# A graph layer on one core: the first node tile made alone, its own small table, the bias product after that of h, and counts that get ahead over 20 steps

## The chip, the cores and the metric

The kernel runs on one core of one Trainium2 chip. A core has TensorE (PE, with weight loads as PEld), VectorE (DVE), ScalarE (ACT), GpSimd (POOL) and SyncE (SP, which here only issues DMAs). The metric is device microseconds of one execution. The median of three runs of the kernel before is 5252.87 us (5247.94 to 5257.49).

## The reference

Node features `x` (12500 x 128) go through a graph layer with a residual. There are 412500 edges, sorted by destination node `dst`:

```
h    = relu(layernorm(x)) @ W_in2f
Wij  = (ssp(f_ij @ W_f1 + b_f1) @ W_f2 + b_f2) * rcut_ij      # 20 -> 128 -> 128 per edge
agg  = segment_sum(h[dst] * Wij, src)                          # idx_j = dst, idx_i = src
out  = x + ssp(agg @ W_o1 + b_o1) @ W_o2 + b_o2                # ssp(z) = softplus(z) - log 2
```

Since `dst` is sorted, the rows of h that 512 edges in a row need lie close together: about 15.5 nodes per 512 edges. The sources are in no order, so the messages have to be spread over all nodes.

## The kernel before, in words

**Making h.** `make_h(q)` (L332) makes h for a quad of four tiles of 128 nodes, in steps parted by `yield`: load of x, statistics (DVE, and two activations on ACT); scaling (DVE); transposes (PE) and relu (ACT); product with `win` (PE) and first bfloat16 part (ACT); the rest after that part (`left`, DVE) and second part (ACT); third part (DVE) and stores. Three bfloat16 parts stand for one float32. The stores go to HBM tables (`tables`, L129): table 0 holds the first quad, the others overlapping stretches, and a chunk reads from the one that `table_of` names (0 for chunks 0 to 8), so that it can read before later quads are there.

**Edges in chunks.** A chunk is 512 edges, a group four chunks; there are 806 chunks. For chunk k the following is issued. `rows` (L614): SP reads a start row from `shifts` into a register and loads 32 rows of the h table (`near`). `window` (L757): DVE compares relative destinations (`rel`, loaded per group in twelve-step advance) with row numbers, giving 0/1 matrices `at`. `pick` (L775): PE multiplies `at` by `near`, giving h rows for the edges; ACT scales them by rcut (`picked`, L784, gives `hg`). `hidden`, `hidden_log`, `hidden_end` (L663 to L685): the first layer of the edge net, two chunks at a time, on PE, ACT (three activations) and DVE (`r`). `value` (L764): second layer on PE, with the bias product of `ones_b` and `bf12_p` last in the sum. `message` (L793): DVE multiplies `v` and `hg` into `o`, and POOL scatters it to HBM by four indirect DMAs, one per 128 edges. Slots of the scatter come from counts: `blocks` (L687, DVE, `inb`), `rank` (L695, PE, sum over the edges so far in `free`), `rank_end` (L712, DVE, `top` and, for the first three groups, three small operations per chunk). `free` is one PSUM tile that each count adds to, so a count waits for `rank_end` of the one before.

**Collecting.** Slots are zeroed ahead in segments (L1127). After each segment, `Collect` (L818) loads them, compares and adds them up on DVE and PE beside later chunks; the last segment and the output layer (`finish`) come after the last scatter.

**Order.** The whole program is written out in order by hand (`manual_schedule`, L1096): each engine and each DMA queue runs its instructions in program order. Before the loop come `constants` (L254), the first quad, and the pieces of chunk 0. Then `step(k)` (L954) from k = -1 issues what is due: `part(name, upto, make)` makes all chunks up to a limit. In step k the message is that of k, pick and value are those of k + 1, hidden that of k + 4. For k under 10 (`steady` false) the end of the counts (`slots`) comes ahead of the message, later after it; the count limit `upto` (L1001) grows by half a chunk more per step until it is 6 ahead. After each step both first `make_h` generators move on by one step; from k = 6 (`NEXT - 3` is 5) `side` makes the later quads, one per nine steps, and the starts and relative destinations of later chunks. `rows` are held back to chunk `NEXT` until the second quad is stored.

`biases` and `bias_parts` (L304, L311) form the fixed second-layer bias b_f1 W_f2 + b_f2 (the hidden layer is kept without b_f1, which `nbf1` and this product make up for) and cut it into three bfloat16 rows of `bf12_p`.

Of the kernel before, what the change touches and what calls it, by code (L numbers as in the profile page):

```python
# [41 lines left out]
def gnn_kernel(  # L42
# [84 lines left out]


    tables = [(0, QN)]  # L129
# [4 lines left out]
    for c in range(NC):  # L134
        n = c * CH * N // n_edges
        table_of.append(0 if n < QN - NEAR - P else min(n // QN, NQ - 1) + 1)
# [46 lines left out]
    def load_x(q):  # L183
        n = min(QT, NTILE - q * QT)
        full = min(n, N // P - q * QT)
        xb = ln.tile([P, QT, P], F32, name="xb")
        if full < n:
            nc.vector.memset(xb[:, full:n, :], 0.0)
            nc.sync.dma_start(xb[:N % P, full, :], x[q * QN + full * P:N, :])
        if full:  # L190
            nc.sync.dma_start(xb[:, :full, :], x[q * QN:q * QN + full * P, :]
# [62 lines left out]
    def constants():  # L254
# [3 lines left out]
        first_load(0)  # L258
        nc.sync.dma_start(win, w_in2f)

        for j in range(NCHUNK):
            nc.sync.dma_start(wf1[32 * j:32 * j + RBF, :], w_f1)

        nc.scalar.preload_act_table_set("natural_log_exp_and_others")
        nc.scalar.dma_start(bf1, b_f1[:, None])
        nc.scalar.dma_start(wf2, w_f2)
        nc.scalar.dma_start(bf2, b_f2[None, :].to_broadcast([P, P]))
# [4 lines left out]
        prow_i = early_room[:WP, rows_at + 5 * NC:rows_at + 5 * NC + 1].bitcast(I32)  # L272
# [7 lines left out]
        nc.gpsimd.memset(ones_b, 1.0)  # L280
        nc.gpsimd.memset(bf12_p, 0.0)
# [9 lines left out]
        nc.vector.memset(bad, 0.0)  # L291
        nc.vector.memset(rel[:, NPART - 1, :], 0.0)
        nc.vector.memset(ones, 1.0)
        nc.vector.memset(none, 0.0)

        for t in range(QT):
            nc.vector.memset(turn[:, :, t:t + 1], -1.0 if t % 2 else 1.0)
        nc.vector.tensor_scalar(prow_i, prow_i, 7, None, op0=ALU.logical_shift_right)
        nc.vector.tensor_copy(prow, prow_i)
# [3 lines left out]

    def biases(psum):  # L304

        nc.vector.tensor_scalar(nbf1, bf1, -1.0, None, op0=ALU.mult)
        b12 = psum.tile([P, QT, P], F32, name="b12", tag="acc")[:, 0, :]
        nc.tensor.matmul(b12, bf1.to_broadcast([P, P]), wf2, start=True, stop=True)
        nc.vector.tensor_add(bf12, b12, bf2)

    def bias_parts():  # L311

        left = bf12[:3, :]
        for k in range(3):
# [926 lines left out]
```

## Time and profile before

| what | value |
|---|---|
| median of three runs | 5252.87 us |
| the profiled execution's own time | 4236.61 us |
| its span, first to last instruction | 4234.9 us |
| mean granted TensorE clock | 0.882 |
| POOL busy | 3095.9 us (73%), 3246 instructions |
| PE, DVE, ACT busy | 3371.9 us (80%), 3352.9 us (79%), 2329.8 us (55%) |
| DMA moved | 820.92 MB, mean 194 GB/s |
| first and last scatter start | 26.1 and 4106.6 us |

The profile is one execution; its own time is 1016 us less than the median of the runs, so durations from it are set against its own time. A row of the table of groups gives line, engine, operation, output and inputs, then the busy total in us, the mean ns of one instruction, and the engine's idle time just before them with what ended most of it. A timeline row gives start and duration in us, then in brackets the idle time before it and its releaser; `SPq` are DMA issues on SP. "issue" is time in which the engine waited for nothing that the profile shows. DMA issue rows show issuing time only, landing comes later.

### The profile page before, as it was taken

The numbers are of one execution on the slowest core, as the hardware profiler recorded it, in microseconds if no ns is written. First come the engines' busy times: TensorE is split into PE (matmuls) and PEld (weight loads), VectorE is DVE, ScalarE is ACT, GpSimd is POOL, SyncE is SP. The second block draws the span as 40 slices with busy tenths as digits, with TensorE's granted clock in tenths as the row PEclk, the third lists the DMA queues.
The fourth block names the chain that finished last, engine by engine and source line by source line (L and its number), as shares of the span: only waits on it lengthen the run. The fifth ranks groups of instructions, "written<-read, shape, count | busy, mean of one in ns | idle before, by whom it ended". The sixth has DMA issues, their size and how long they took to land. (4 is left out here: it accounts for less than half of the span.)

```text
span 4234.9 us, 73728 instructions
## 1 busy us (share of the span) xinstructions
PE 3371.9 (80%) x22378; PEld 2543.6 (60%) x22378; DVE 3352.9 (79%) x6752; ACT 2329.8 (55%) x4686; POOL 3095.9 (73%) x3246
## 2 busy tenths in 40 slices
PE   6766666666666666689998899898898988888888
PEld 4444444444444444467777777777776777767777
DVE  8877766776666656678888888888888998999978
ACT  5665565655555555555555555555555555555535
POOL 5777777777777777777777777777777777777760
PEclk9877877877777777789999999999999999999999
DMA  5765555555444454366787777877787768767667
GB/s 171 213 192 180 176 175 177 157 159 159 126 118 132 121 164 125 107 193 210 229 269 213 216 212 211 267 229 218 214 243 234 229 203 270 234 203 204 184 183 232
DMA packets 515591, 820.92 MB, mean 194 GB/s; under 512 B 177075, under 2 KB 312871, under 8 KB 515187
## 3 DMA queue, kind: packets, MB, share of 16 engines
q1 hardware_dynamic: 411586, 602.85, 49.2%
q0 software_dynamic: 103168, 213.15, 15.3%
q8 instruction: 181, 2.97, 0.3%
q14 instruction: 224, 1.83, 0.1%
q10 hardware_dynamic: 432, 0.13, 0.0%
HBM read 419.09 MB, written 396.64 MB: 193 GB/s over the span
## 5 line engine op out<-in xcount | busy, mean ns | idle before, releaser
L804 POOL DMA_INDIRECT slots<-o,slot x3224 | 3092.5, 959 | 1010.8 <-issue 770.3
L769 PE MATMUL v<-wf,r 128*128 128x128 f32 x6448 | 1066.6, 317 | 540.7 <-DVE o L800 539.1
L769 PEld LDWEIGHTS v<-wf,r 128*128 128x128 f32 x6448 | 924.7, 221 | 590.3 <-DVE o L800 571.2
L789 ACT ACTIVATE hg<-picked,rcut 128x128 f32<-128x128 f32 x3224 | 907.7, 368 | 630.9 <-PE picked L780 292.5
L866 PEld LDWEIGHTS acc<-to,m 128*128 128x128 f32 x8132 | 1017.2, 201 | 235.9 <-issue 142.0
L866 PE MATMUL acc<-to,m 128*128 128x128 f32 x8132 | 1078.8, 289 | 32.5 <-DVE to L853 22.1
L675 ACT ACTIVATE a<-z,bf 128x1024 f32<-128x1024 f32 x403 | 450.4, 1118 | 853.5 <-PE z L668 853.0
L668 PE MATMUL z<-f,wf 20*128 20x512 f32 x1612 | 527.2, 734 | 224.8 <-DVE r L684 223.3
L853 DVE TENSOR_TENSOR to<-count_ps,m 128x512 f32<-128x512 f32 (+3 forms) x824 | 641.8, 804 | 65.6 <-DMA m<-slots 34.7
L800 DVE TENSOR_TENSOR o<-v,hg 128x512 f32<-128x512 f32 x806 | 550.5, 683 | 48.8 <-PE v L771 25.0
L798 DVE COPY o<-place 128x8 f32<-128x8 f32 x403 | 77.0, 191 | 610.6 <-DMA slots<-o,slot 609.9
L760 DVE TENSOR_TENSOR at<-count_ps,rel 96x512 bf16<-96x512 f32 x806 | 545.7, 677 | 0.0
L684 DVE SCALAR_TENSOR_TENSOR r<-z,nbf,a 128x1024 f32<-128x1024 f32 x403 | 513.9, 1275 | 21.1 <-ACT a L677 21.1
L677 ACT ACTIVATE a<-a,half 128x1024 f32<-128x1024 f32 x403 | 462.8, 1148 | 13.1
L713 DVE TENSOR_REDUCE top<-free 128x4 f32<-128x392 f32 x806 | 446.7, 554 | 8.1 <-PE free L708 8.1
L689 DVE TENSOR_TENSOR inb<-count_ps,blk 128x392 f16<-128x392 f32 x806 | 447.4, 556 | 0.0
L676 ACT ACTIVATE a<-a 128x1024 f32<-128x1024 f32 x403 | 426.0, 1057 | 12.8
L780 PEld LDWEIGHTS <-at 96*128 96x128 bf16 x3224 | 256.0, 105 | 251.1 <-DVE at L760 104.0
L668 PEld LDWEIGHTS z<-f,wf 20*128 20x128 f32 x1612 | 138.8, 210 | 409.6 <-DVE r L684 362.2
L780 PE MATMUL picked<-near,at 96*128 96x128 bf16 x3224 | 343.2, 234 | 32.1 <-DVE at L760 26.8
L771 PE MATMUL v<-bf_p,ones_b 128*128 128x512 bf16 x806 | 353.3, 438 | 0.0
L741 PE MATMUL free<-inb,rest_of 128*128 128x392 f16 x806 | 302.9, 376 | 12.6 <-DVE top L713 12.6
(112 smaller groups left out, 1428.2 us busy)
## 6 DMA issues: line engine op xcount, KB each, us to landing
m<-slots SPq DMA_DIRECT2D x311, 387.0 KB
m<-slots SPq DMA_DIRECT2D x317, 258.0 KB
rel<-rel_d SPq DMA_DIRECT2D x202, 384.0 KB
m<-slots SPq DMA_DIRECT2D x172, 322.5 KB
slots<-o,slot POOLq DMA_INDIRECT x3224
slots<-zero SPq DMA_DIRECT2D x96, 387.0 KB
slots<-zero SPq DMA_DIRECT2D x64, 516.0 KB
f<-in_f_t SPq DMA_DIRECT2D x404, 80.0 KB
```

The costliest lines, as they stand in the source:

```text
L668: nc.tensor.matmul(z[:, k, :], wf1[rows, :], self.f[rows, :], start=True, stop=True)
L675: nc.scalar.activation(a, z, AF.Abs, bias=bf1)
L677: nc.scalar.activation(a, a, AF.Ln, bias=half, scale=0.5)
L684: nc.vector.scalar_tensor_tensor(r, z, nbf1, a, op0=ALU.max, op1=ALU.add)
L760: nc.vector.tensor_tensor(at, prow_ps.to_broadcast([WP, CH]), self.rel[:, c, :], op=ALU.is_equal)
L769: nc.tensor.matmul(v[:, i, :], r[:, i * P:(i + 1) * P], wf2, start=i == 0, stop=False, skip_group_check=True)
L780: nc.tensor.matmul(ps[:, i, :], at[:, i * P:(i + 1) * P], near, start=True, stop=True)
L789: nc.scalar.activation(hg[:, i, :], ps[:, i, :], AF.Copy, scale=self.rcut[:, j:j + 1])
L800: nc.vector.tensor_mul(o[:, :, :P], v, hg)
L804: put = nc.gpsimd.indirect_dma_start(out=views[j % VIEWS], out_offset=bass.IndirectOffsetOnAxis(ap=self.slot[:, j:j + 1], axis=0), in_=o[: ...
L853: nc.vector.tensor_tensor(to[:, :n, :], count_ps[:, None, :].to_broadcast([P, n, P]), self.m[u][:, :n, P:].to_broadcast([P, n, P]), op=ALU ...
L866: nc.tensor.matmul(self.acc[b // QT][:, i, :], m[:, j, :P], to[:, j, :], start=t == 0, stop=t == self.seg.tiles(b) - 1)
```

## The change

The first `make_h` makes one tile, the second the other three of the first quad, the third and later ones a quad each (`made_h`). A new table 0 holds the first tile's 128 rows and serves chunks 0 to 4; the first quad's table serves chunks 5 to 22; later tables are as before, numbered one higher. `served()` gives the last chunk whose table has been stored in program order, in place of `NEXT`. Of the constants, `win` and two of the four copies of `w_f1` are loaded by ACT's queue; `wf2`, `bf2`, the first destinations, the next three tiles of x and the other two copies move to SP behind the first group's source indices, and the first `rel` store and load behind the statistics. DVE's constants move into `more_constants` and `window_rows`, and three memsets to the late loads. `bias_parts` is gone: the bias product comes after h's on PE, and its three parts are cut on all partitions, with `ones_b` now zero but for rows 0, 32 and 64. `shift` comes after h is stored. In the loop the non-steady form lasts 20 steps, the window and the counts get ahead over those 20 steps, the third `make_h` starts at step 4, and the side work at step 12. What is computed stays the same.

```diff
-    tables = [(0, QN)]
+    made_h = [(0, 1), (1, QT - 1)]
+    made_h += [(t, min(QT, NTILE - t)) for t in range(QT, NTILE, QT)]
+    tables = [(0, P), (0, QN)]
...
     table_of = []
     for c in range(NC):
         n = c * CH * N // n_edges
-        table_of.append(0 if n < QN - NEAR - P else min(n // QN, NQ - 1) + 1)
+        table_of.append(0 if n <= P - 2 * WR else 1 if n < QN - P - WR
+                        else min(n // QN, NQ - 1) + 2)
...
         early[0] = load_x(0)
         part_load(0)
-        first_load(0)
-        nc.sync.dma_start(win, w_in2f)
-        for j in range(NCHUNK):
-            nc.sync.dma_start(wf1[32 * j:32 * j + RBF, :], w_f1)
         nc.scalar.preload_act_table_set("natural_log_exp_and_others")
+        nc.scalar.dma_start(win, w_in2f)
+        for j in range(2):
+            nc.scalar.dma_start(wf1[32 * j:32 * j + RBF, :], w_f1)
         nc.scalar.dma_start(bf1, b_f1[:, None])
...
-        nc.gpsimd.memset(ones_b, 1.0)
-        nc.gpsimd.memset(bf12_p, 0.0)
+        nc.gpsimd.memset(ones_b, 0.0)
+        for k in range(3):
+            nc.gpsimd.memset(ones_b[32 * k:32 * k + 1, :], 1.0)
...
+    def more_constants():
+        nc.vector.scalar_tensor_tensor(after, ident, BIG, after, op0=ALU.mult, op1=ALU.add)
+        nc.vector.tensor_scalar(rest_of, after, -1.0, 1.0, op0=ALU.mult, op1=ALU.add)
+        for t in range(QT):
+            nc.vector.memset(turn[:, :, t:t + 1], -1.0 if t % 2 else 1.0)
         nc.vector.memset(bad, 0.0)
+    def window_rows():
+        nc.vector.tensor_scalar(prow_i, prow_i, 7, None, op0=ALU.logical_shift_right)
+        nc.vector.tensor_copy(prow, prow_i)
+    def biases(psum):
+        b12 = psum.tile([P, QT, P], F32, name="b12", tag="acc")[:, 0, :]
+        nc.tensor.matmul(b12, bf1.to_broadcast([P, P]), wf2, start=True, stop=True)
+        yield
+        nc.vector.tensor_scalar(nbf1, bf1, -1.0, None, op0=ALU.mult)
+        nc.vector.tensor_add(bf12, b12, bf2)
+        nc.scalar.activation(bf12_p, bf12, AF.Copy)
+        yield
+        nc.vector.tensor_sub(bf12, bf12, bf12_p)
+        for r in (slice(P // 4, P // 2), slice(P // 2, P)):
+            nc.scalar.activation(bf12_p[r, :], bf12[r, :], AF.Copy)
+        yield
+        r = slice(P // 2, P)
+        nc.vector.tensor_sub(bf12[r, :], bf12[r, :], bf12_p[r, :])
+        nc.scalar.activation(bf12_p[r, :], bf12[r, :], AF.Copy)
...
-    def bias_parts():
-        left = bf12[:3, :]
-        for k in range(3):
-            part = ln.tile([3, P], BF16, name="bias_part", bufs=1)
-            nc.vector.tensor_copy(part, left)
-            nc.vector.scalar_tensor_tensor(bf12_p[:3, :], part, ident[:3, k:k + 1],
-                                           bf12_p[:3, :], op0=ALU.mult, op1=ALU.add)
-            if k < 2:
-                nc.vector.tensor_sub(left, left, part)
...
+        for j, ((b, rows), table) in enumerate(zip(tables, h3_t)):
+            lo = max(0, b // P - t0)
+            hi = min(n, (b + rows) // P - t0)
...
                 nc.sync.dma_start(
                     table[r:r + (hi - lo) * P, :].rearrange("(c p) f -> p c f", p=P),
                     hb[:, lo:hi, :, :].rearrange("p c k f -> p c (k f)"))
-                if b + rows == QN:
+                if i_h == j < 2:
+                    stored[0] = t0 + n
                     yield
...
+        stored[0] = t0 + n
         yield
...
+        def rel_load(group):
+            g = group.g
+            if g == 0:
+                rel_store(0)
+            nc.sync.dma_start(group.rel, rel_d[g * NCHUNK:(g + 1) * NCHUNK, :][None, :, :]
+                              .to_broadcast([WP, NCHUNK, CH]))
...
+                if i % SB == 0:
+                    src_i = edge.tile([P, SB * TG], I32, name="src_i")
+                    nc.sync.dma_start(src_i[:, :w], src_t[:, cols])
+                if g == 0:
+                    nc.sync.dma_start(wf2, w_f2)
+                    nc.sync.dma_start(bf2, b_f2[None, :].to_broadcast([P, P]))
+                    first_load(0)
                 if g % NB == 0:
                     f = edge.tile([P, NB, CH], F32, name="f")
                     for j in range(NCHUNK):
+                        if g == 0 and j == 2:
+                            early[1] = load_x(1)
+                            for k in range(2, NCHUNK):
+                                nc.sync.dma_start(wf1[32 * k:32 * k + RBF, :], w_f1)
                         nc.sync.dma_start(f[32 * j:32 * j + RBF, :, :],
                                           f_t[g:g + NB, j].rearrange("b k n -> k b n"))
...
+                if g:
+                    rel_load(self)
...
-        NEXT = table_of.index(1) - 1
+        def served():
+            for c in range(NCH):
+                start, rows = tables[table_of[c]]
+                if stored[0] < min(NTILE, ceil_div(start + rows, P)):
+                    return c - 1
+            return NCH
         LG, LW, LR, LZ = 12, 6, 6, 4
+        RAMP = 20
...
-            steady = k >= 10
+            steady = k >= RAMP
             group((k + LG) // NCHUNK)
-            part("rows", min(k + LW, 2 * k + 3, NEXT if k < NEXT - 3 else NCH), rows)
+            part("rows", min(k + LW, 2 * k + 3, served()), rows)
...
             if not steady:
-                part("window", k + 1 if k < 1 else k + 2 if k < 6 else k + 3, window)
+                part("window", k + 1 + max(0, k) * 2 // (RAMP - 2), window)
             part("blocks", made["rank"] + 2, blocks)
             part("end", min(k + LZ - 2, made["log"]), pairs(hidden_end))
             if steady:
                 part("window", k + 3, window)
-            part("pick", k + 1 if k < 8 else k + 2, pick)
+            part("pick", k + 1 if k < RAMP - 2 else k + 2, pick)
...
-            upto = max(made["rank"], min(k + LR, k + 1 + (k + 1) // 2))
+            upto = max(made["rank"], min(k + LR, k + 1 + (k + 1) * (LR - 1) // RAMP))
...
-                if i % 9 == 0 and 2 + i // 9 < NQ:
-                    quads.append(make_h(2 + i // 9, psum))
+                if i % 9 == 0 and 3 + i // 9 < len(made_h):
+                    quads.append(make_h(3 + i // 9, psum))
...
         with tc.manual_schedule():
             constants()
+            bias = biases(psum)
+            h = [make_h(i, psum) for i in range(3)]
+            group(0)
+            next(h[0])
+            window_rows()
             nc.scalar.activation(count_ps, places, AF.Copy)
             nc.scalar.activation(prow_ps, prow, AF.Copy)
-            h = [make_h(q, psum) for q in range(2)]
-            next(h[0])
+            columns = groups[0].column_parts()
             next(h[0])
             relative(0)
+            rel_load(groups[0])
+            next(h[0])
+            more_constants()
+            next(h[0])
+            next(bias)
+            next(h[0])
+            next(bias)
+            part("hidden", 0, hidden)
+            next(h[0])
+            next(bias)
             shift(0)
-            group(0)
-            early[1] = load_x(1)
-            next(h[0])
-            part("hidden", 0, hidden)
+            part("rows", 1, rows)
+            next(columns)
+            next(bias, None)
+            next(columns, None)
             part("blocks", 0, blocks)
-            next(h[0])
             ready = ranks(0)
             next(ready)
-            next(h[0])
             part("log", 0, hidden_log)
+            part("window", 0, window)
             next(ready, None)
             made["rank"] = 0
-            next(h[0])
-            part("rows", 1, rows)
-            biases(psum)
             part("end", 0, hidden_end)
-            part("window", 0, window)
...
                 step(k, now)
-                for m in h:
-                    next(m, None)
-                if k > NEXT - 3:
+                next(h[0], None)
+                next(h[1], None)
+                if k == 1:
+                    next(h[1], None)
+                if k > 3:
+                    next(h[2], None)
+                if k > 11:
                     next(aside, None)
             summed[0].add(summed[1])
             summed[0].keep()
```

## The prediction

> **What bounds the kernel now.** I read the page's table of groups first, for the engine whose work fills the span, then windows cut at the first and last scatter, then POOL's timeline and the head's. The costliest row is POOL's scatter (busy, mean ns of one, idle before it):
>
> ```profile
> L804 POOL DMA_INDIRECT slots<-o,slot x3224 | 3092.5, 959 | 1010.8 <-issue 770.3
> ```
>
> The idle time is nearly all 0.30 us after each scatter, so one costs 0.96 + 0.30 = 1.26 us and a chunk (4 of them) 5.05 us. The waits of POOL name one other releaser of size (us in total, times, longest):
>
> ```profile
> POOL slots L804 <- DVE o L800: 46.8, 63, 21.8
> ```
>
> and after 200 us no single wait of POOL is over 0.3 us. Four windows (length, then busy time of each engine with its count, TensorE clock, DMA share, GB/s):
>
> ```profile
> 0.00:26.11 26.11, 11.33 (x36) 6.32 (x36) 20.16 (x85) 8.95 (x16) 3.46 (x22) 1.00 0.49 133
> 26.11:83.19 57.08, 39.46 (x211) 24.70 (x211) 44.74 (x117) 34.27 (x73) 38.86 (x40) 0.91 0.70 203
> 83.19:4107.60 4024.41, 3212.17 (x21379) 2421.01 (x21379) 3185.22 (x6385) 2224.87 (x4498) 3053.60 (x3184) 0.88 0.65 193
> 4107.60:4234.90 127.30, 108.90 (x755) 91.62 (x753) 102.77 (x168) 61.69 (x100) 0.00 (x0) 0.97 0.76 228
> ```
>
> In the third, 3184 scatters take 4024.41 us, 1.264 each: POOL never waits. So the end is (start of chunk 10's scatters, 83.19) + 4024.4 + a tail of 127.3 that the edit leaves alone. The edit can only move the 83.19. That is 26.11 of head, ten chunks at 5.05 (50.5) and 6.6 of stalls. The stalls show in POOL's own timeline as starts over 1.26 after the last:
>
> ```profile
> 26.11 1.13 POOL L804 DMA_INDIRECT slots<-o,slot  x1 [21.83 <-DVE o L800]
> ...
> 33.90 0.96 POOL L804 DMA_INDIRECT slots<-o,slot  x1 [2.87 <-DVE o L800]
> ...
> 41.38 0.96 POOL L804 DMA_INDIRECT slots<-o,slot  x1 [2.75 <-DVE o L800]
> ...
> 62.99 0.96 POOL L804 DMA_INDIRECT slots<-o,slot  x1 [1.12 <-DVE o L800]
> ```
>
> (0.30 of each is the usual gap: 2.6, 2.45 and 0.8 are lost, the rest in crumbs.) The head's chain in the timeline:
>
> ```profile
> 0.81 0.45 SPq L191 DMA_DIRECT2D xb<-in_x  x1
> ...
> 4.45 0.29 DVE L343 BATCH_NORM_STATS2 st<-xb 128x6 f32<-128x128 f32 x1 [0.58 <-DMA xb<-in_x]
> ...
> 16.31 0.39 SPq L384 DMA_DIRECT2D h<-hb  x1
> ...
> 18.94 1.52 SPq L623 DMA_DIRECT2D near<-h  x2
> ...
> 20.66 0.59 PE L780 MATMUL picked<-near,at 96*128 96x128 bf16 x4 [5.27 <-DMA near<-h]
> ...
> 25.13 0.68 DVE L800 TENSOR_TENSOR o<-v,hg 128x512 f32<-128x512 f32 x1
> ```
>
> A whole quad of x becomes h before anything can be picked; then v(0) ends at 23.49, and o(0) stands 1.6 us behind the second quad's statistics on DVE (23.50 to 25.09).
>
> **The Trainium skill.** "TensorE: Matmul & The Clock Gate", Part 1: the array starts at half rate and a busy window of about 3.4 us releases it. Here the 128x512 bias matmul takes 0.63 us until 38 us and 0.38 from then, returning to 0.63 in places; the trace agrees, though PE was busy for over 3.4 us before (20.7 to 25.5) without release. "DMA: Bandwidth & Descriptors", Anatomy of one DMA: about 2 us of fixed cost, mostly the write receipt. The trace: rel stored at 9.06, its reload goes at 10.80 (1.74 us); h stored at 16.31, near loads go at 18.94 (2.63). Same page, "Issuing engines are not separate DMA queues": issuing from another engine saves only issue time; here that is 0.4 to 0.7 us per DMA on SP.
>
> **Part by part: the head.** The first x load falls from 256 to 64 KB: landing 4.4 becomes about 3.2 (between 2.8, two us after issue, and 4.4). Statistics and scaling of one tile instead of four save 3 x 0.39 and 3 x 0.28 on DVE; transposes and h matmuls 3 x 0.3 and 3 x 0.52 on PE; ACT and DVE passes halve from 0.6-0.7 to 0.3. The z matmuls (2.08), which stood ahead of h's at 8.91, move behind them. My times: scaled x 5.3, h in PSUM 6.6, left 7.5, last bf16 part 8.25. The win and two wf1 loads go to ACT's queue: 1.5 us of issue before its first activation at 3.9, free. SP now issues 13 DMAs in group 0 until 7.7, stores rel, and waits 1.74 for it; the h store, in order behind, goes at 9.8, not 8.3. near goes at 12.1 and lands at 13.8 (1.7, as 18.94 to 20.6). Cover for that: DVE. After 8.25 it has a bias step (0.25), shift (1.3), columns (0.9 + 2.15), bias (0.25), inb (0.55) and the window (0.7) to 14.6, so near's landing costs nothing unless it is 0.8 later. Then top 0.57, small ops 0.6, r 1.28: 17.0. The bias parts (8 DVE ops, 20.31 to 22.62) are gone, for three subtractions, an add and five ACT copies in gaps; constants of 0.8 us go to the gap at 6 to 7 while h is made; about 0.2 us of added POOL memsets lie before its idle time; three memsets (0.55) go to late loads, under a saturated POOL. The new table costs one more store of the first tile on SP (0.4) in step -1, where nothing on SP is urgent before near(2). If the cover of these pieces fails, each costs its own length, 0.2 to 1.3 us. v(0) needs r: 17.05 + 2.5 = 19.55. DVE meanwhile does two inb (1.0) and statistics of three tiles (1.2). o(0) at 19.6, **first scatter 20.6: 5.5 us earlier.**
>
> **The ramp.** Chunk 1: z(2) follows v(0) on PE, 19.5 to 21.6; its three activations (3.4) end at 25.0; r(2) 26.3; second step of the three tiles 1.5; rank end 1.1; o(1) runs 28.9 to 29.6, scatter at 29.9, against 33.90. ACT is the long pole here: hg(1) stands behind those activations and ends at 26.6. From here each step before 20 has the order o, window, pick, v, rank, rank end, o. In the old order the window was one or two chunks ahead from step 1; now, to step 8, the window of k+1 is made in step k and PE waits for it: o 0.6 + window 0.7, pick through rank 1.9 (45.95 to 47.83) with the fast clock, 3.5 (26.47 to 29.97) with the slow, rank end 0.57 + 0.6: 4.35 us a step fast, 6.0 slow. A step with two ranks costs 1.15 more (69.62 to 70.77). Against it stand fewer ranks and windows: to step 6, two of each less, about 4.6 us of DVE. With the slow clock to 38 us, as now: o(2) 35.7, o(3) 41.4 (PE also has the three tiles' transposes and h matmuls in step 1), o(4) 47.9 after the two ranks of step 3.
>
> Then the added wait. Chunks 0 to 4 read the one-tile table, 5 to 22 the first quad's, stored at the end of step 3 (hb at 46.7). near(5) is issued in step 4, and pick(5) is in step 4 too. On SP between them: store 0.45, a zero fill 0.43, four f loads 1.45, rel 0.33, the register load about 1.2, then landing 1.7: 5.8 us, so 52.5. (The store alone can hold it: 54.76 to 59.49 now, 4.7.) PE would be ready at 49.2, so it waits 3.3; behind it stand v(5) and rank(6), and DVE's rank end and o(5) wait for those: 57.2. Behind near(5) on SP stand near(6) to (10) and the other stores, not urgent. The next quad's statistics (1.7) meet the two ranks of step 7: 7.2 us for that step, 6.4 for step 8 with its scaling. Scatters start (old in brackets): chunk 2 36.7 (41.38), 3 42.4 (46.43), 4 48.9 (51.67), 5 57.5 (57.13), 8 73.4 (73.09), 9 79.8 (78.14), 10 84.9 (83.19). So stalls grow from 6.6 to about 13.8, and the profiled execution would go from 4236.6 (span 4234.9, 1.7 around it) to about 4238.3. After chunk 10 a fast step is under 5.05 and POOL keeps its lead. The side work (later quads, starts) begins at step 12 instead of 6: that costs nothing, since chunk 23 is the first to need the second quad, its load may wait to step 17, and the quad is stored at step 12; if it slipped past 17, the price would again be near's 4 to 6 us.
>
> **To the median.** The runs' median, 5252.87, is 1016 us above the profiled execution. No row says where that is; as only POOL is without slack, the least strained reading is slower scatters: 1016/3224 = 0.315 each, 6.31 per chunk (an estimate). Then the old stalls are 1.5 + 1.2, chunk 10 at 92.0; the new: chunk 1 waits 3.0, chunk 2 0.5, chunk 5 2.4, chunk 10 at 89.7. That is -2.3 us, and the forecast: 5252.9 - 2.3 = **5250.6**. About 0.2% (10.5 us) is what a measurement of this kernel can tell from no change.
>
> **Rivals.** (a) Likeliest, 0.74: head gain mostly handed back in the ramp, -7 to +7 us. (b) 0.14: the array clock is released by 25 to 30 us and near(5) lands in time. For it: PE's work is denser early. Against: SP's queue. Then stalls fall to about 2: 5.5 + 4.6 = 10 us, more where x lands early: 5242. (c) 0.12, slower: the window-then-pick order with an array clock that stays slow through step 8. Then the five steps from 4 to 8 cost 1.65 more each (6.0 for 4.35), 8.2 us on top of the +1.7 of the profile's own sum: +10, 5263. For it: the clock does fall back in the trace (0.63 us bias matmuls at 57 and 64), and waiting on near(5) leaves PE idle for six us. Against: it was fast for most of 39 to 87. It decides once more than half of those steps are slow and scatters run at 1.26; at 1.58 a chunk's 6.31 covers a slow step and it vanishes. That the tables don't do what they say would need nodes off by over 30 rows; a chunk starts 15.5 nodes after the last, so no chance is given.
>
> Range: 5242 to 5262, taking in (b)'s and most of (c)'s place and both ends of near(5) (0 to 5 us) and x (2.8 to 4.4).
>
> **What would show it.** First scatter at 20 to 22; a wait of PE's pick on near of 2 to 5 us near 50; stalls of POOL at chunks 1 and 5; chunk 10 starting within 4 us of 83.2; then 1.264 per scatter and a tail of 127. Wrong if POOL stalls between steps 10 and 20, or chunk 10 starts before 78.

## The result, and the profile after

The changed kernel takes 5258.03 us (median of 12 runs, 5243.28 to 5269.89); the kernel before, beside it, 5257.86 us (12 runs, 5246.72 to 5270.32). The ratio is 0.9997, with a 95% interval of 0.9983 to 1.0011: no difference that can be measured. The forecast was 5250.6 us, most likely no change.

The profiled execution of the changed kernel took 5267.65 us (span 5265.8). The kernel before was profiled at 4236.61, and the experiments point to why the two profiles stand 1000 us apart: the same kernel takes 4251 to 4253 us in some groups of runs (the quick kind of chip below) and 5258 to 5328 in others (the slow kind), and by their times the two profiles belong to one kind each. So totals of the two profiles are not compared here. Single steps up to about 36 us can be: chunk 2 starts at 35.77 in this profile and at 35.86 and 35.89 in two of the quick kind, while chunk 3 is already 0.6 to 1.1 us apart. In the medians of the shortened kernels below, runs more than 1.5% above the fastest of the same kernel are left out (two of six for the kernel before, three of six each for the new ramp alone and for everything together).

First the rows of the table of groups for the scatter and for `o`, in the changed kernel (L833 is the old L804, L829 the old L800; busy, mean ns, idle before):

```profile
L833 POOL DMA_INDIRECT slots<-o,slot x3224 | 3095.0, 960 | 2024.5 <-DVE o L829 1128.0
...
L829 DVE TENSOR_TENSOR o<-v,hg 128x512 f32<-128x512 f32 x806 | 552.5, 686 | 1279.4 <-remote 781.3
```

One scatter costs what it did before (960 ns against 959). On this chip POOL waits 1128 us for `o` instead of 46.8, and DVE waits before `o` for something whose releaser the trace doesn't have ("remote"). The prediction had read the missing 1016 us as slower scatters; that reading is wrong.

The head, from the timeline (start, duration, engine, idle time before and releaser):

```profile
2.91 0.29 DVE L351 BATCH_NORM_STATS2 st<-xb 128x6 f32<-128x128 f32 x1 [1.94 <-DMA xb<-in_x]
...
10.76 0.38 SPq L392 DMA_DIRECT2D h<-hb  x1
...
13.97 1.53 SPq L647 DMA_DIRECT2D near<-h  x2
...
15.76 0.59 PE L809 MATMUL picked<-near,at 96*128 96x128 bf16 x4 [0.99 <-DVE top L765]
...
19.82 0.69 DVE L829 TENSOR_TENSOR o<-v,hg 128x512 f32<-128x512 f32 x1 [0.46 <-PE v L800]
```

x lands at 2.9 (4.45 before), h is stored at 10.76 (16.31), `near` goes at 13.97 (18.94), and pick waits only 0.99 us where it waited 5.27. `o` starts at 19.82, 5.3 us earlier. POOL's own timeline shows where that goes:

```profile
20.81 1.13 POOL L833 DMA_INDIRECT slots<-o,slot  x1 [15.75 <-DVE o L829]
...
29.86 0.96 POOL L833 DMA_INDIRECT slots<-o,slot  x1 [4.14 <-DVE o L829]
...
35.77 0.96 POOL L833 DMA_INDIRECT slots<-o,slot  x1 [1.18 <-DVE o L829]
...
59.52 0.95 POOL L833 DMA_INDIRECT slots<-o,slot  x1 [7.67 <-DVE o L829]
...
81.87 0.96 POOL L833 DMA_INDIRECT slots<-o,slot  x1 [4.22 <-DVE o L829]
```

These are the first scatters of chunks 0, 1, 2, 5 and 8. The largest stalls that the kernel before didn't have stand at chunks 5 and 8 (one of 3.34 us stands at chunk 7 between them). The one at chunk 5, in the full timeline:

```profile
44.55 0.41 SPq L392 DMA_DIRECT2D h<-hb  x1
...
50.16 6.30 SPq L647 DMA_DIRECT2D near<-h  x6
...
53.99 0.58 PE L809 MATMUL picked<-near,at 96*128 96x128 bf16 x4 [9.99 <-DMA near<-h]
```

The three tiles are stored, then SP issues a zero fill, four f loads and rel, and the load of chunk 5's rows goes out 5.6 us after the store. It takes 3.8 us more to be there. PE has stood still for 9.99 us by then.

### The profile page after: what moved, and what is told of

The parts are those of the page before. It is cut to its first block, busy times and chain, and to the rows that moved or that the text cites. A ratio compares the mean times of both kernels' runs of the same rounds, so it can differ in the third digit from the quotient of the medians.

```text
span 5265.8 us, 73740 instructions
## 1 busy us (share of the span) xinstructions
PE 3797.0 (72%) x22378; PEld 2798.9 (53%) x22378; DVE 3375.1 (64%) x6752; ACT 2332.5 (44%) x4695; POOL 3099.1 (59%) x3250
## 5 line engine op out<-in xcount | busy, mean ns | idle before, releaser
L833 POOL DMA_INDIRECT slots<-o,slot x3224 | 3095.0, 960 | 2024.5 <-DVE o L829 1128.0
L798 PE MATMUL v<-wf,r 128*128 128x128 f32 x6448 | 1192.1, 342 | 832.8 <-DVE o L829 764.5
L798 PEld LDWEIGHTS v<-wf,r 128*128 128x128 f32 x6448 | 1032.3, 243 | 912.5 <-DVE o L829 813.4
L829 DVE TENSOR_TENSOR o<-v,hg 128x512 f32<-128x512 f32 x806 | 552.5, 686 | 1279.4 <-remote 781.3
L895 PE MATMUL acc<-to,m 128*128 128x128 f32 x8132 | 1211.9, 303 | 217.2 <-issue 144.4
L895 PEld LDWEIGHTS acc<-to,m 128*128 128x128 f32 x8132 | 1112.9, 213 | 477.3 <-issue 354.9
L697 PE MATMUL z<-f,wf 20*128 20x512 f32 x1612 | 566.3, 785 | 220.8 <-DVE r L713 122.1
L742 DVE TENSOR_REDUCE top<-free 128x4 f32<-128x392 f32 x806 | 448.0, 556 | 113.1 <-remote 55.7
L809 PEld LDWEIGHTS <-at 96*128 96x128 bf16 x3224 | 274.5, 111 | 379.6 <-issue 226.0
L809 PE MATMUL picked<-near,at 96*128 96x128 bf16 x3224 | 376.9, 245 | 120.1 <-issue 65.2
L800 PE MATMUL v<-bf_p,ones_b 128*128 128x512 bf16 x806 | 382.6, 475 | 1.5 <-issue 1.5
L770 PE MATMUL free<-inb,rest_of 128*128 128x392 f16 x806 | 326.5, 405 | 33.5 <-DVE top L742 21.9
L737 PE MATMUL free<-inb,after 128*128 128x392 f16 x806 | 323.8, 402 | 5.8 <-DVE inb L718 4.1
```

Source lines behind the costliest of these rows:

```text
L697: nc.tensor.matmul(z[:, k, :], wf1[rows, :], self.f[rows, :], start=True, stop=True)
L798: nc.tensor.matmul(v[:, i, :], r[:, i * P:(i + 1) * P], wf2, start=i == 0, stop=False, skip_group_check=True)
L809: nc.tensor.matmul(ps[:, i, :], at[:, i * P:(i + 1) * P], near, start=True, stop=True)
L829: nc.vector.tensor_mul(o[:, :, :P], v, hg)
L833: put = nc.gpsimd.indirect_dma_start(out=views[j % VIEWS], out_offset=bass.IndirectOffsetOnAxis(ap=self.slot[:, j:j + 1], axis=0), in_=o[: ...
L895: nc.tensor.matmul(self.acc[b // QT][:, i, :], m[:, j, :P], to[:, j, :], start=t == 0, stop=t == self.seg.tiles(b) - 1)
```

## The experiments

Ten of the runs use a shortened program: it ends after step 47 and leaves out all chunks after, the last collecting and the output layer (the one-line edit below, the code after the loop removed, one store of a tile in its place). Times of 290 us show single microseconds that 4250 hide. Two runs are of whole kernels. The runs came in four groups, each on one chip; the first group and the last run had the same chip. Two profiles of one kernel can lie well apart: the profile before, 4236.61 us, is below all 57 runs of the kernel before on quick chips (4239.31 at the least), so chunk starts are set side by side here, and what a change is worth is taken from medians.

```diff
-            for k in range(-1, max(NCH, max(units) + 1)):
+            for k in range(-1, 48):
```

**Both kernels, shortened**, with the edit above alone.

> The kernel before, cut to its first 48 chunks (what leaves out: all later chunks, the collecting of slots and the output layer; one tile of messages is written in place of the output), so that a few us in the head are a per cent or more of the time. Head 26.1 and ramp as in the full kernel's profile, then 38 chunks at 5.05 us: about 275 us if scatters run without gaps, about 320 us if the 1016 us between the profile before and the runs are spread evenly over all chunks (6.3 us each). This is the mark that the other short kernels are measured against.

> The changed kernel cut in the same way. My theory (5.3 us of head gained, handed back by PE's wait for the rows of chunk 5 and by steps of 6 us at the slow TensorE clock): within 5 us of the short kernel before, rather above it than below. Rival one (the head's gain stays, the later stalls lie under scatters that have gaps anyway): 4 to 6 us less. Rival two (the new ramp costs well over what the head gains): 5 to 12 us more.

Measured: 289.58 us before (median of four; all six span 288.53 to 295.31, with a median of 291.18), 295.83 after (5 runs, 294.98 to 297.49): the change costs 6.25 us here, or 4.65 with all six. On this chip the whole kernel before takes 4251.5. Starts of the chunks' first scatters:

| chunk | before | after | predicted for after |
|---|---|---|---|
| 0 | 25.96 | 20.81 | 20.6 |
| 1 | 33.78 | 29.86 | 29.9 |
| 2 | 41.04 | 35.89 | 36.7 |
| 3 | 46.09 | 41.88 | 42.4 |
| 4 | 51.41 | 48.81 | 48.9 |
| 5 | 56.87 | 61.63 | 57.5 |
| 8 | 72.70 | 78.94 | 73.4 |
| 9 | 77.75 | 85.03 | 79.8 |
| 10 | 82.79 | 90.45 | 84.9 |

The change is 5.15 us ahead at chunk 0, still 2.6 at chunk 4, then 4.8 behind at chunk 5 and 7.7 at chunk 10. Behind chunk 10 the distance stays (7.9 at the 44th chunk). The profiled execution of the kernel before is its quickest, 288.53, and that of the change took 296.52, so the table shows 1.7 us more than the medians. The timeline of the shortened changed kernel around chunk 5:

```profile
46.82 0.41 SPq L392 DMA_DIRECT2D h<-hb  x1
...
47.87 2.29 SPq L621 DMA_DIRECT2D f<-in_f_t  x4
...
50.20 0.33 SPq L594 DMA_DIRECT2D rel<-rel_d  x1
...
52.00 5.84 SPq L647 DMA_DIRECT2D near<-h  x6
...
56.09 0.58 PE L809 MATMUL picked<-near,at 96*128 96x128 bf16 x4 [9.52 <-DMA near<-h]
...
60.67 0.68 DVE L829 TENSOR_TENSOR o<-v,hg 128x512 f32<-128x512 f32 x1
...
61.63 0.96 POOL L833 DMA_INDIRECT slots<-o,slot  x1 [8.07 <-DVE o L829]
```

From store to pick it is 9.3 us: 5.2 to the issue and 4.1 to the landing. The load stands behind rel's, which moves 384 KB: in the packet records of this trace rel's 4096-byte packets run from 51.24 to 54.57, those of the f loads end at 53.63, and the first of `near`'s 256-byte packets starts at 53.44, 1.4 us after its issue (1.0 in the head of the kernel before). The windows of the same trace (length, busy times and counts of PE, PEld, DVE, ACT, POOL, then TensorE clock, DMA share, GB/s) show the DMA engines 81% busy just before it goes out and PE at half clock while it waits:

```profile
50.00:52.00 2.00, 0.00 (x0) 0.00 (x0) 1.26 (x2) 0.00 (x0) 1.62 (x2) 0.50 0.81 214
52.00:56.10 4.10, 0.01 (x1) 0.05 (x2) 0.00 (x0) 0.00 (x0) 1.25 (x2) 0.50 0.54 167
```

**The three tiles a step earlier.** The second `make_h` moves on twice in step 0 as well, so that the first quad is stored before step 3.

```diff
-                if k == 1:
+                if k in (0, 1):
                     next(h[1], None)
```

> The short changed kernel with the second make_h moved on twice after step 0 as well, so that the three tiles are stored at the end of step 2 and the rows of chunk 5 are loaded in step 3, one step before they are picked. My theory: PE's wait of about 10 us before pick(5) goes, POOL's stall at chunk 5 falls from 7.4 us to under 3, and the time is 4 to 7 us below the short changed kernel. Rival (the stall only moves to the next steps, which run at the pace of the DVE and PE chain): less than 2 us.

Measured, on the same chip: 293.81 us (5 runs, 292.89 to 294.34), 2.0 below the changed kernel, 4.2 above the one before. Chunk 5 starts at 55.86 with a stall of 0.66, 5.8 us earlier than in the change; but chunk 8 at 76.04 and chunk 10 at 87.42 are only 2.9 and 3.0 earlier. The early tiles themselves cost 2.0 us at chunk 2 (37.91 for 35.89). Where the rest goes is seen at chunk 8:

```profile
71.00 0.57 DVE L742 TENSOR_REDUCE top<-free 128x4 f32<-128x392 f32 x1 [2.63 <-PE free L737]
...
72.07 0.28 DVE L351 BATCH_NORM_STATS2 st<-xb 128x6 f32<-128x128 f32 x1
...
73.67 0.53 DVE L742 TENSOR_REDUCE top<-free 128x4 f32<-128x392 f32 x1
...
75.08 0.69 DVE L829 TENSOR_TENSOR o<-v,hg 128x512 f32<-128x512 f32 x1
...
76.04 0.96 POOL L833 DMA_INDIRECT slots<-o,slot  x1 [3.72 <-DVE o L829]
```

Two counts end in this step (L742 twice) with the statistics of the next quad between them, and `o` stands behind all of it. So the wait for `near` is real and removable, and a second stall three chunks on takes back half of what its removal gives. Against the kernel before, this kernel is 1.0 us ahead at chunk 5 (55.86 for 56.87) and 4.6 behind at chunk 10 (87.42 for 82.79), with no wait for `near` between. From 42 to 92 us PE's picks wait 13.0 us for windows, in seven waits, and PE runs at a lower clock than in the kernel before: 0.91 there from 60 to 80 us, 0.67 in this kernel, and 0.59 in the changed kernel with the old ramp (the next run). The three rows, in this order, have the columns of the rows above:

```profile
60.00:80.00 20.00, 13.27 (x82) 8.31 (x81) 17.60 (x47) 12.13 (x25) 14.70 (x16) 0.91 0.77 204
...
60.00:80.00 20.00, 11.54 (x53) 7.59 (x53) 14.84 (x46) 8.41 (x19) 11.31 (x13) 0.67 0.61 189
...
60.00:80.00 20.00, 14.60 (x65) 9.24 (x64) 14.02 (x42) 11.33 (x25) 11.74 (x13) 0.59 0.64 200
```

The bias product, 0.38 us at the full clock, takes 0.63 in this kernel for all chunks from 5 to 10 (0.38 for chunks 8 to 10 in the kernel before).

**The old ramp in the changed kernel.** `RAMP` 10 and the formulas of before for windows and counts.

> The short changed kernel with the windows, picks, counts and the non-steady form of the kernel before (10 steps); its head, tables and the wait for chunk 5 stay. My theory: windows one step ahead take 1.3 us out of each step up to 8, so chunks 6 to 10 start earlier, against more counts in steps 3 to 8: 1 to 4 us below the short changed kernel. Rival (spreading the counts is what helps): 2 to 5 us above it.

Measured: 297.41 us (5 runs, 294.46 to 297.9), 1.6 above the changed kernel with overlapping runs: no gain. Chunk 5 at 60.28, chunk 10 at 90.28, against 61.63 and 90.45. With the wait for `near` left in, the order of the ramp makes no difference at chunk 10; the clock is low here too, though windows are made ahead and counts lead as in the kernel before.

**The whole changed kernel on another chip.** No edit; three more kernels ran beside it on a chip on which the kernel before takes 4250.88 us (27 runs, 4239.31 to 4260.33).

> The changed kernel whole, unaltered, beside the kernel before on one chip, timed in more rounds. The short kernels' medians differ by 4.65 us. If scatters run without gaps on this chip too (the kernel before near 4250 us, as beside the short kernels), my theory: the whole kernel keeps that and is 3 to 9 us slower (0.07 to 0.2%), its chunk 10 starting near 90. If the kernel before takes near 5255 here, no more than 3 us of difference either way is expected, since gaps come at all chunks. Rival (what the ramp loses is made up later): within 1 us.

Measured: 4254.07 us (22 runs, 4248.61 to 4266.75), ratio 1.0013 with an interval of 1.0006 to 1.0021. Here the change is slower, by 2.6 to 8.9 us, and the 6.25 of the shortened pair lie in that interval. In its profile (4266.04 us, near the slow end of these runs) chunk 5 starts at 61.62 and chunk 10 at 93.14, against 57.13 and 83.19 in the profile before, and the bias products of chunks 4 to 9 all take 0.63 us.

**The new ramp in the kernel before.** Twenty steps, windows and counts as in the change, the head and the tables of before.

```diff
-            steady = k >= 10
+            steady = k >= 20
...
-                part("window", k + 1 if k < 1 else k + 2 if k < 6 else k + 3, window)
+                part("window", k + 1 + max(0, k) * 2 // 18, window)
...
-            part("pick", k + 1 if k < 8 else k + 2, pick)
+            part("pick", k + 1 if k < 18 else k + 2, pick)
...
-            upto = max(made["rank"], min(k + LR, k + 1 + (k + 1) // 2))
+            upto = max(made["rank"], min(k + LR, k + 1 + (k + 1) * (LR - 1) // 20))
```

> The short kernel before with the new ramp alone: windows, picks, counts and the non-steady form over 20 steps; head, tables and row loads as before. Theory that the loss lies in the wait for chunk 5 and in the third make_h meeting the two counts of step 7: little change here, within 2 us of the short kernel before. Rival (the ramp itself costs: pick waits for a window of the same step, some 1.3 us a step with the fast clock, more with the slow): 3 to 7 us more.

Measured: 293.63 us (median of three; all six span 291.38 to 299.0). The profiled execution, the quickest of them, has chunk 0 at 26.07, chunk 2 at 39.80 (41.04 in the kernel before), chunk 5 at 55.67 (56.87), chunk 8 at 74.30 with a stall of 3.05, and chunk 10 at 85.67 (82.79). So the ramp gains 1.2 us early, as fewer counts should, and loses 4 at steps 7 to 9. There the clock is low again: 0.50 on average from 66 to 87 us, where the shortened kernel before has 0.98. By the medians the ramp costs 4.1; the runs scatter so much, and the kernel before was run on another chip, that only the place is safe: at chunk 8, without any wait for `near`. Two counts in step 7 are not enough to explain it: the kernel before ends two counts in its step 7 as well, and `o(7)` to `o(8)` takes 4.24 us there and 7.79 here.

**The third `make_h` later.** With the three tiles early, the next quad starts at step 9 instead of 4.

```diff
-                if k > 3:
+                if k > 8:
                     next(h[2], None)
```

> The short changed kernel with the three tiles stored a step earlier, as in the run before this one, and besides the third make_h begun at step 9 instead of 4, so that its statistics fall in step 12 and not in step 7 with its two counts. Theory: the stall of 3.7 us at chunk 8 and the 1.3 at chunk 9 go, chunk 10 starts near 83, and the time is 3 to 5 us below that run (near 290). Rival (the work is only moved to where it hurts as much): no change, 293 to 294.

Measured: 293.60 us (5 runs, 292.78 to 294.33), 0.2 below the kernel without this edit (on the other chip). Chunk 8 starts at 75.43 for 76.04 with a stall of 2.38 for 3.72, chunk 10 at 86.13 for 87.42, the 44th at 255.57 for 255.80. So the rival came true: the statistics at step 7 are worth 0.6 to 1.3 us at chunks 8 to 10, and next to nothing of it is left later.

**Everything together, and the hidden layer a step later.** Early tiles, late third `make_h`, the old ramp, and the hidden layer's end and start one step back so that `o(1)` doesn't stand behind the next pair's activations.

```diff
-            part("end", min(k + LZ - 2, made["log"]), pairs(hidden_end))
+            part("end", min(k + (LZ - 2 if k > 7 else 1), made["log"]), pairs(hidden_end))
...
-            part("hidden", k + LZ, pairs(hidden))
-            if k < 4:
-                part("log", k + LZ, pairs(hidden_log))
+            part("hidden", min(k + LZ, made["end"] // 2 * 2 + 3), pairs(hidden))
+            if 0 <= k < 4:
+                part("log", min(k + LZ, made["hidden"]), pairs(hidden_log))
```

> All that the runs so far point to, on the short changed kernel: three tiles stored a step earlier, third make_h from step 9, the ramp of the kernel before (windows ahead from step 1), and the end of the hidden layer moved one step back, with its activations behind the picked rows of chunk 1, so that message 1 doesn't wait for the second pair. Theory: chunk 1 starts at 27 to 28 instead of 29.9, chunk 10 near 77 to 79, and the time is 4 to 7 us below the short kernel before (284 to 287). Rival (the chain of DVE and PE at the slow clock takes it all back): no better than the short kernel before.

Measured: 309.81 us (median of three; all six span 307.74 to 315.95), some 16 above the run before: a miss. In the profiled execution, the slowest of the six, chunk 1 does start early, at 26.73 (29.86), but chunk 2 only at 42.46:

```profile
36.10 1.11 ACT L704 ACTIVATE a<-z,bf 128x1024 f32<-128x1024 f32 x1 [7.41 <-PE z L697]
...
39.39 0.47 ACT L380 ACTIVATE hb<-hps 128x384 bf16<-128x384 f32 x1
39.90 0.56 DVE L383 TENSOR_TENSOR left<-hps,hb 128x384 f32<-128x384 f32 x1 [6.12 <-ACT hb L380]
...
41.51 0.68 DVE L829 TENSOR_TENSOR o<-v,hg 128x512 f32<-128x512 f32 x1
...
42.46 0.96 POOL L833 DMA_INDIRECT slots<-o,slot  x1 [10.98 <-DVE o L829]
```

The activations that were in the way of chunk 1 (three of them, 36.10 to 39.49) now stand ahead of the three tiles' `hb` on ACT; DVE's `left` waits 6.12 us for it, and the count and `o(2)` are queued behind `left`. One wait went and a longer one came. That is only part of the loss: against the run before, chunk 10 is 8.4 us later (94.53 for 86.13) and the 44th chunk 17.9, since POOL goes on waiting behind chunk 10. The mean clock from 26 to 87 us is 0.55; what holds the later chunks was not followed up.

**Parts of the ramp alone**, in the kernel before: only the window later; then only the counts, the pick and the twenty steps, with the windows ahead as before. And **the changed kernel mended otherwise**: chunk 5 stays on the one-tile table (whose 128 rows hold what it needs), and the windows are made ahead as before.

```diff
-                part("window", k + 1 if k < 1 else k + 2 if k < 6 else k + 3, window)
+                part("window", k + 1 if k < 8 else k + 3, window)
```

```diff
-        table_of.append(0 if n <= P - 2 * WR else 1 if n < QN - P - WR
+        table_of.append(0 if n <= P - WR - 16 else 1 if n < QN - P - WR
...
-                part("window", k + 1 + max(0, k) * 2 // (RAMP - 2), window)
+                part("window", k + 1 if k < 1 else k + 2 if k < 6 else k + 3, window)
```

> The short kernel before with one edit: up to step 7 the window of chunk k + 1 is made in step k, just ahead of its pick, as in the changed kernel; counts and the rest as before. Theory (the late window is what the new ramp loses by: PE waits for it in each step, and its pauses keep the TensorE clock slow): at least two thirds of the 5 us by which the whole new ramp is above the short kernel before, so 294 to 297, with PE waiting for the window in each of steps 1 to 7. Rival (the loss lies in the counts or in the non-steady form to step 20): under 1.5 us above it.

> The short kernel before with the rest of the new ramp: counts get ahead over 20 steps, the non-steady form and single picks last to steps 20 and 18, windows one or two steps ahead as before. Theory: within 1.5 us of the short kernel before, or a little below. Rival: 3 to 6 us above it.

> The short changed kernel with two edits: the one-tile table serves chunk 5 too (a start of up to 80 rows instead of 64), so that the first rows from the three tiles are picked in step 5 and not in step 4, and windows are ahead as in the kernel before; the counts over 20 steps stay. Theory: POOL's stall of 8 us at chunk 5 falls to under 3 in all at chunks 5 and 6, chunk 10 starts at 80 to 84, and the time is 7 to 10 us below the short changed kernel, at or below the short kernel before (286 to 290). Rival (what is spared at chunk 5 returns as slow steps to chunk 10): 292 to 295.

Measured: 340.87, 346.22 and 343.20 us (5 runs each). The chip was of the slow kind (the whole kernel before takes 5327.92 us on it), and neither shortened kernel ran on it without these edits, so these stand against each other only. Late windows alone are 5.35 us quicker than the slower counts alone, against the theory that the late windows are the costly part; which part of the ramp costs on the quick kind of chip was not tried and stays open. In the third, chunk 5 starts at 52.36, where the changed kernel has 59.52 on such a chip; chunk 8 starts at 77.78 (81.87) and chunk 10 at 88.91 (93.25). The stall at chunk 5 is gone, but one of 4.14 stands at chunk 6 and one of 6.73 at chunk 8, so chunk 10 is behind the 80 to 84 of the theory.

**The mended kernel, whole.** The edits are the last two above: only chunk 5 moves to the one-tile table, the tables of the later chunks stay.

> The whole kernel, with the first table serving chunks 0 to 20 less one step, so that chunk 5 is served by the one-tile table of the second kind and waits for no load that was issued just before, and with the windows made ahead as in the kernel before; all else as in the change. On chips where the kernel before takes about 4251: theory (the change loses its head start at the load of chunk 5 and at the slow-clock steps behind it): stall ahead of chunk 5 under 3 us, chunk 10 between 80 and 84, and the time 3 to 8 us below the kernel before. Rival (the slow steps take back whatever is ahead): chunk 5 near 52 but chunk 10 at 86 or later, and the time within 2 us of the kernel before or above it. On chips where the kernel before takes 5260 or more: chunk 5 near 52, chunk 10 near 89 as in the short kernel, and the time within 6 us of the kernel before; then the two are not told apart.

Measured, on a chip of the quick kind: 4250.68 us (14 runs, 4241.41 to 4259.67), the kernel before 4253.43 (19 runs, 4243.32 to 4265.2), ratio 0.9992, interval 0.9982 to 1.0002. Chunk 5 starts at 52.29 and chunk 10 at 85.55, between what the two theories gave. From its timeline:

```profile
45.24 0.41 SPq L392 DMA_DIRECT2D h<-hb  x1
...
50.23 4.85 SPq L647 DMA_DIRECT2D near<-h  x5
...
52.29 0.96 POOL L833 DMA_INDIRECT slots<-o,slot  x1 [0.33 <-DVE o L829]
...
55.26 0.61 PE L809 MATMUL picked<-near,at 96*128 96x128 bf16 x4 [3.03 <-DMA near<-h]
...
60.90 0.96 POOL L833 DMA_INDIRECT slots<-o,slot  x1 [3.87 <-DVE o L829]
```

The wait for the quad's rows is now at chunk 6: `near` goes 5.0 us after the store and is there 5.0 later. One chunk of delay took the stall from 8.13 (the whole changed kernel) to 3.87. The interval includes 1, so this kernel isn't shown to beat the one before. It doesn't overlap that of the change (0.9982 to 1.0002 against 1.0006 to 1.0021), each against its own runs of the kernel before.

## Why the prediction was right or wrong

**The head: right.** First scatter predicted at 20.6, measured at 20.81. Inside it, h was stored about 1 us and `near` issued 1.9 us later than worked out (10.76 and 13.97 for 9.8 and 12.1), and DVE's chain covered nearly all of it: pick waited some 1 us and `o` came 0.2 late. The part with the least margin was rightly named.

**Chunks 1 to 4: right.** Within 0.9 us at each of them in the table above. ACT was the long pole of chunk 1 as told.

**Chunk 5: the mechanism right, the size wrong.** The prediction gave 5.8 us from store to landing: issue after 4.1, landing after 1.7. Measured: 5.2 and 4.1, 9.3 in all. The 1.7 was taken from a load in the head, with nothing ahead of it; the prediction counted rel at its 0.33 us of issue and not the 384 KB that it moves. The packet records above have `near` start among the last packets of the f loads and of rel, but no run took rel away by itself, so this cause is argued, not shown. The Trainium skill, "DMA: Bandwidth & Descriptors", Latency and other measured facts, gives the HBM's latency as 0.2 us on average and 2 us at high load, which could be a part of it; the trace has 2.4 us more for the landing, in a stretch where the DMA engines were 81% busy just before, and does not tell the two apart. Predicted chunk 5: 57.5, measured 61.63 (61.62 in the whole kernel). That the wait is what holds chunk 5 is shown by the two kernels that remove it (55.86 and 52.29).

**The steps behind it: right in one trace, too short in the other.** In the shortened kernel `o(7)` to `o(8)` took 7.3 us (70.64 to 77.98; predicted 7.2), the next 6.1 (6.4), and `o(5)` to `o(7)` 10.0 us for the 8.7 of two quick steps. In the whole changed kernel of the quick kind the steps from `o(5)` to `o(9)` took 5.5, 5.9, 9.0 and 6.1 us for 4.35, 4.35, 7.2 and 6.4. There chunk 10 comes 8.2 us later than predicted (93.14 for 84.9): 4.1 from the longer wait at chunk 5 and 4.2 from these steps.

The difference goes with the clock. The Trainium skill, "TensorE: Matmul & The Clock Gate", Part 1, has the array fall to half rate after an idle window of about 3.4 us. The shortened trace agrees in part: the 9.52 us of idle were followed by a clock of 0.50 and a bias product of 0.63 us at 58.27, then 0.38 at 63.18; but it is 0.63 again at 68.24, though PE had stood for no more than 2.52 us at a time since. In that trace the bias products of chunks 5 to 10 are mixed (0.63, 0.38, 0.63, 0.38, 0.63, 0.63). In the whole changed kernel of the quick kind they are 0.63 from chunk 4 to chunk 9, in the profile of the result from chunk 5 to chunk 10: every step from 4 to 8 is slow. Rival (c), given a chance of 0.12, had said this, and about +10 us with it; chunk 10 is 9.95 us behind the profile before. But half of the 8.2 us is the longer wait at chunk 5 and not the slow steps, and by the medians the end is only 3.2 us later.

Two of the signs that the prediction named failed: PE's pick waits 9.5 to 10.1 us for `near` and not 2 to 5, and chunk 10 starts 7 to 10 us behind 83.2 and not within 4.

**Behind chunk 10: right on one kind of chip, up to chunk 770.** On the quick kind POOL keeps its pace so far, but for crumbs of 1 us or less; in the profile of the whole changed kernel ten waits of 0.6 to 2.5 us follow at chunks 771 to 802, 11 us in all. The profile before has none over 0.5 us there. That execution took 12 us more than the median of its runs, so they may be its own. On the kind of chip that the runs of the result used, POOL waits for `o` throughout, 414 times. This is what the prediction named as the sign that it is wrong, and for that kind it is.

**The median: right by luck.** The profile's own sum was +1.7 us; measured on the quick kind are +3.2 (medians of whole kernels) and +6.25 (shortened). The step to the runs' median read 1016 us as 0.315 us on every scatter and so turned +1.7 into -2.3. Scatters still take 0.960 us, and by all signs the 1016 us are those of another kind of chip. With that step failed, nothing of the prediction explains why the two kernels come out equal there (0.9997); that its range held is owed to a gain and a loss that nearly cancel on both kinds.

**Where the gain went.** 5.2 us of head are real. They are given back at chunk 5 (a table that is needed soon after it is stored, through a queue with other loads in it) and in the steps behind it, above all step 7. Removing the first alone returns 2.0 us of 6.25. For the second the place is shown, by the kernel without the wait and by the new ramp in the kernel before, and so is that these steps run at half clock for longer than in the kernel before; a slow step costs 1.65 us more by the prediction's own count. Why the clock stays low is open: with the new ramp PE waits for windows made in the same step, but putting the old ramp back into the changed kernel, with the wait left in, returned nothing, and the clock was as low there.

## What to carry to other kernels

A head start is worth what is left of it where the engine that sets the end stops waiting for good: follow the start times of its work item by item, here chunk by chunk to the tenth, before adding anything up, and read the TensorE clock of each step with them. When a load depends on a store a few steps back, take its landing time from a place in the trace with the same traffic ahead of it, bytes and not issues, since an idle head shows 1.7 us where 4.1 come due. When a profile and the runs differ by a quarter, don't spread the difference over the busiest engine: the two may come from different chips, and then any sum that uses it is a guess.

## What the runs showed of the hardware

**Two kinds of chip.** The kernel before takes 4251.5, 4250.9 and 4253.4 us in three groups of runs on two chips, and 5257.9 and 5327.9 in two other groups. That it is the chip, and not something that changes with time, is not shown, though one chip was quick twice. The same program was profiled on both kinds. PE's line and those of its neighbours in the page, the changed kernel on the slower kind:

```profile
PE 3797.0 (72%) x22378; PEld 2798.9 (53%) x22378; DVE 3375.1 (64%) x6752; ACT 2332.5 (44%) x4695; POOL 3099.1 (59%) x3250
```

and on the quicker:

```profile
PE 3412.6 (80%) x22378; PEld 2569.0 (60%) x22378; DVE 3354.6 (79%) x6752; ACT 2327.7 (55%) x4695; POOL 3097.9 (73%) x3250
```

DVE, ACT and POOL work as long in both, to within 0.6%. PE is 384 us busier for the same 22378 matmuls, at a mean granted clock of 0.807 for 0.867, and its idle time is 617 us longer. The slower profile has 439 waits, from 71 us on and through the whole program, whose releaser is not in the trace ("remote"; 781.3 us of DVE's ahead of `o` alone); the three whole profiles of the quick kind have none. PE is the one engine that is slower itself; whether it also stands still in these waits, and why, stays open.

**A dependent load under traffic.** From the issue of `near` to the first matmul that uses it: 1.7 to 1.8 us at the head, 3.8 to 5.0 at 50 us, over the traces shown here.

**The TensorE clock behind chunk 5.** The traces' clock records have only 0.50 and 1.00. In the shortened kernel before the mean is 0.98 from 66 to 87 us, with the new ramp alone 0.50, and in the whole changed kernel of the quick kind 0.51. In that kernel `o(5)` to `o(9)` take 26.5 us, where the prediction gave 22.3. Ahead of a trace's first clock record (at 39 us in the profile before) a window shows 1.00, though the bias products of that stretch take 0.63 us: the 1.00 in the first of the prediction's four windows is no full clock.
